# Layer 3's convolution, gate, u and u·B of 28 of 32 chunks placed between layer 1's tiles

## The chip, the cores and the metric

The kernel runs on one NeuronCore of a Trainium2 chip. Its engines work side by side, each through its own instruction stream in order: TensorE (PE, with its weight loads PEld), VectorE (DVE), ScalarE (ACT), GpSimd (POOL), and SyncE (SP), which here only issues DMAs. Times are device microseconds (us) of whole executions, the median of several, and one more execution is taken by the hardware profiler. Lower is better.

## The reference

Four layers are applied in turn to x of shape (4, 64, 64, 128): four images of 4096 pixels with 128 channels, all in float32.

```python
# layer 0: neighbourhood attention (7x7 windows, 4 heads of 32), gated, plus x
# layer 1: group norm, then attention of all 4096 pixels over all 4096, plus x
h = group_norm(x, gn_scale, gn_bias); hf = h.reshape(B, N, C)
q, k, v = hf @ wq + bq, hf @ wk + bk, hf @ wv + bv
w_ = softmax(einsum('bqd,bkd->bqk', q, k) * C ** -0.5, axis=2)
x = x + (einsum('bqk,bkd->bqd', w_, v) @ wo + bo)
# layer 2: per pixel, with one sum over each image row
out = ((x @ W_left + b_left) + (x @ W_eq + b_eq)) * sum_over_row(x @ W_right + b_right)
x = layer_norm((out * sigmoid(x @ W_gate + b_gate)) @ W_out + b_out + x)
# layer 3: a gated scan in four directions over 256 channels
xb, z = split(x @ Win)                     # 256 and 256 channels
xb = silu(depthwise_conv3x3(xb) + conv_b)  # u of the scan
xs = stack([xf, xf[::-1], xt, xt[::-1]])   # rows, rows backwards, columns, columns backwards
dt, Bs, Cs = split(xs @ Wxproj)            # 8, 1 and 1
delta = softplus(dt @ dt_weight + dt_bias)
x_t = exp(delta*A) * x_(t-1) + delta*u*B;  y_t = x_t*C + u*D
out = norm((y0 + y1 + y2 + y3) * silu(z)) @ Wout
```

## The kernel before, in words

`layers_0_to_2` (L91) takes one image b after the other. `layer_0(b)` is a generator that does the neighbourhood attention block by block; the additive masks for windows (`bias_m`, three tiles for inner rows of blocks, and an edge tile tagged "be" for the first and last row of blocks) stay in SBUF, and `edge_bias(0)` for the next image is loaded when layer 0 of this one has ended. `layer_1(b)` (L483) does the attention over all pixels in 32 tiles of 128 queries. In the turn of tile i it does four things. `soften(i-1)` takes the maximum of the previous tile's scores: three halvings on DVE (L554), a transpose on PE (L556), a reduction (L558), a diagonal (L560), a broadcast by PE (L562), the subtraction on DVE (L565) and the exponential on ACT (L566). `score(i)` does 8 groups of 4 matmuls (L542) into one of four PSUM buffers (tag "s"), each copied to SBUF by ACT (L545), with running maxima on DVE (L547, L549). `value(i-2)` (L572) multiplies the exponentials with v, its groups alternating with the scores on PE. `finish(i-2)` (L576, L577) divides by the sum.

After each tile `between(i)` (L677) is called. From i = 6 on it does a quarter of a chunk of layer 2: chunk n and part are `divmod(i - 6, 4)`, the parts being `turn`, `mix`, `add` and `norm`, and a chunk is four tiles, 512 pixels. `norm` stores the chunk's result, transposed, to DRAM (`x3_d`, L663). After layer 1's last tile, four more turns end layer 2 while the next image's layer 0 starts.

`layer_3` (L693) begins when all images are done. For each of 32 chunks (4 images of 8) `project` (L807 to L816) loads x from `x3_d` ("x3T"), multiplies it with Win into xb (copied to SBUF by ACT) and z (Silu on ACT, stored to `zf_d`). `convolve` (L817 on) forms the 3x3 convolution in PSUM: three of the nine taps on PE as matmuls with weights that were multiplied with the taps beforehand (L825), six on DVE as multiply-adds onto PSUM (L832). ACT applies Silu to it (u, L837), and D·u goes into the accumulators `zs` through ACT and POOL (L841 to L845). Every fourth chunk multiplies u with Wxproj (L851), which gives dt, B and C ("dbl"). u·B is formed by `times_b` (L882), on POOL an image later, on DVE for the last image, and goes to `ub_d`. The scan stage follows: `deltas` (L937, L945, L947), exponentials (L957) and the scans (L971), then the output stage.

Instructions are put in order by a scheduler; those in `keep_in_program_order` (or `pin`) keep the written order. Each engine then runs its stream in order. All DMAs that are issued with `nc.sync` share SP's stream: one that waits for data holds up those after it. What the numbers of the profile call L556 or L832 are lines of the code below.

Of the kernel before, what the change touches and what calls it, by code (L numbers as in the profile page):

```python
# [29 lines left out]
P = 128  # L30
# [35 lines left out]


@with_exitstack
def conv_seq(ctx, tc, x, mata, matb, cols, rows, rpb, dtw, convw, sel, out):
    nc = tc.nc  # L70
    xf = x.rearrange("b h w c -> b (h w) c")
    of = out.rearrange("b h w c -> b (h w) c")

    dram = ctx.enter_context(tc.tile_pool(name="dram", bufs=1, space=DRAM))
    const = ctx.enter_context(tc.tile_pool(name="const", bufs=1))
    x3_d = [dram.tile([P, L], F32, name=f"x3_d{b}") for b in range(B)]

    ident = const.tile([P, P], F32, name="ident")
    make_identity(nc, ident)
    col = const.tile([P, NCOL], F32, name="col")  # L80
    nc.sync.dma_start(col, cols)

    def cl(name, i=0, n=1, p=P):
        a = COL[name][0] + i
        return col[0:p, a:a + n]

    layers_0_to_2(tc, xf, mata, rows, rpb, ident, cl, dram, x3_d)
    layer_3(tc, of, matb, dtw, convw, sel, ident, cl, dram, x3_d)


@with_exitstack  # L91
def layers_0_to_2(ctx, tc, xf, mata, rows, rpb, ident, cl, dram, x3_d):
    nc = tc.nc
# [59 lines left out]
    for cv, n in enumerate(cols_of):  # L153


        runs = [(0, BC, 0, 3)] if cv == 1 else [(3, BC - 3, 0, 3)] if cv == 0 else [(0, BC - 3, 0, 3)]
        if cv == 0:
            runs += [(q, 1, 0, KS - 1 - q) for q in range(3)]
        if cv == 2:
            runs += [(q, 1, 12, BC - 1 - q) for q in range(BC - 3, BC)]  # L160
        nd = HEADS * (2 * KS - 1)
        for q, count, k, r in runs:
            dst = bass.AP(t_d[cv].tensor, t_d[cv].offset + q * nd * n + k, [[nd * n + 1, count], [n, nd], [1, KS]])
            src = bass.AP(rpb.tensor, rpb.offset + r, [[0, count], [2 * KS - 1, nd], [1, KS]])
            dma(dst, src)


# [89 lines left out]

    bias_m = [wp.tile([P, HEADS * 14 * n], F32, name=f"bias_m{k}") for k, n in enumerate(cols_of)]
    first_edge = edge_bias(0)
# [10 lines left out]
    def layer_0(b, xt, edge_t):  # L270
# [207 lines left out]
        handed[b] = hT, st  # L478
        if b + 1 < B:
            edge_of[b + 1] = edge_bias(0)  # L480

# [121 lines left out]
    def layer_2(b, xt):  # L603
# [61 lines left out]
        return turn, mix, add, norm  # L665

    coming = layer_0(0, x_next, edge_of[0])
    ahead = [x_next]
    for b in range(B):
# [5 lines left out]
        def between(i):  # L675
# [4 lines left out]
            if i >= 6 and n < NCH:  # L680
                parts[part](n)

        layer_1(b, xt, *handed.pop(b), between)
        if b + 1 < B:
# [8 lines left out]
@with_exitstack  # L693
def layer_3(ctx, tc, of, matb, dtw, convw, sel, ident, cl, dram, x3_d):
    nc = tc.nc
# [5 lines left out]

    def stored(name):
        return [[dram.tile([P, L], F32, name=f"{name}{b}_{f}") for f in range(2)] for b in range(B)]

    ub_d, zf_d, y_d = stored("ub_d"), stored("zf_d"), [stored("yn_d"), stored("yt_d")]
    z_d = [dram.tile([P, L], F32, name=f"z_d{f}") for f in range(2)]
    bc_d = [[dram.tile([1, L], F32, name=f"bc_d{b}_{r}") for r in range(3)] for b in range(B)]

# [3 lines left out]

    dbl = wp.tile([P, L], F32, name="dbl")
    dt = wp.tile([P, DI], F32, name="dt")
    nc.sync.dma_start(dt, dtw)
# [47 lines left out]

    RC = CH // W
    taps_pe = [(0, 0), (0, -1), (0, 1)]
    taps_ve = [(-1, 0), (-1, -1), (-1, 1), (1, 0), (1, -1), (1, 1)]
    with pool("u", 22) as up, pool("z") as zp, pool("a", 2) as ap, pool("psB", 2, space=PSUM) as psp:


        zs = [zp.tile([P, L], F32, name=f"zs{f}") for f in range(2)]
        for f in range(2):
            nc.vector.tensor_scalar(
# [23 lines left out]
        xbs = [ap.tile([P, H, W], F32, name=f"xb{f}", tag=f"xb{f}", bufs=1) for f in range(2)]  # L798
        us, bbs = {}, {}

        def region(n, dy, dx):

            return max(0, -dy - RC * n), min(RC, H - dy - RC * n), max(0, -dx), min(W, W - dx)

        def project(b, n):
            x = ap.tile([P, RC, W], F32, name="x3T", tag="x3T", bufs=6)
            nc.sync.dma_start(x, by_rows(x3_d[b][:, bass.ts(n, CH)]))  # L807
            for f in range(2):
                pi = psp.tile([P, RC, W], F32, name="pi", tag="i")
                nc.tensor.matmul(pi, lhsT=mb[:, win + P * f:win + P * f + P], rhs=x, start=True, stop=True)  # L810
                nc.scalar.copy(xbs[f][:, RC * n:RC * n + RC, :], pi)
                pz = psp.tile([P, RC, W], F32, name="pz", tag="i")
                nc.tensor.matmul(pz, lhsT=mb[:, win + DI + P * f:win + DI + P * f + P], rhs=x, start=True, stop=True)
# [5 lines left out]
        def convolve(b, n, x):  # L819
            for f in range(2):  # L820
# [18 lines left out]
                zv = at(zs[f], b, CH * n, CH * n + CH)  # L839
                if b == 0:  # L840
                    nc.scalar.activation(zv, by_rows(u), AF.Copy, scale=d)  # L841
                else:
                    du = ap.tile([P, CH], F32, name="du", tag="du")
                    nc.scalar.activation(du, u, AF.Copy, scale=d)
                    nc.gpsimd.tensor_tensor(zv, zv, by_rows(du), ALU.add)  # L845
            if n % 4 == 3:
# [8 lines left out]
                for g in range(4):  # L855
                    nc.scalar.copy(
                        dbl[32 * b:32 * b + NDBL, bass.ts(n - 3 + g, CH)], pd[32 * g:32 * g + NDBL, :]
                    )
                if b == B - 1:

                    o = 32 * b
                    for g in range(4):
                        pb = psp.tile([P, CH], F32, name="pb3", tag="d")
                        nc.tensor.matmul(
                            pb, lhsT=pick[o:o + NDBL, 0, :], rhs=dbl[o:o + NDBL, bass.ts(n - 3 + g, CH)],
                            start=True, stop=True,
                        )
                        times_b(b, n - 3 + g, pb, nc.vector)
            if n == NCH - 1:
                for r in range(2):  # L870
                    row = 32 * b + RANK + r
                    nc.sync.dma_start(bc_d[b][r], dbl[row:row + 1, :])
                nc.sync.dma_start(cts[b][:, 0, :], by_rows(bc_d[b][1])[0])
                if b < B - 1:
                    turn_c(b, psp.tile([W, W], F32, name="pt3", tag="d"))
                    bbs[b] = zp.tile([P, L], F32, name="bb3", tag="bb3")
                    nc.sync.dma_start(bbs[b], bc_d[b][0][0].partition_broadcast(P))

# [5 lines left out]

        chunks = [(b, n) for b in range(B) for n in range(NCH)]
        xs = {0: project(0, 0)}
        for j, (b, n) in enumerate(chunks):
            if j + 1 < len(chunks):
                xs[j + 1] = project(*chunks[j + 1])
            convolve(b, n, xs.pop(j))  # L890
            if b > 0:
                times_b(b - 1, n, bbs[b - 1][:, bass.ts(n, CH)], nc.gpsimd)
            if (b, n) == (1, NCH - 1):
                load_ub(ub_s[0], 0, 0)
                load_c(cb_s[0], 0, 0)
        for f in range(2):
# [320 lines left out]
```

## Time and profile before

| | |
|---|---|
| median of 3 runs | 3924.59 us (3923.41 to 3926.62) |
| profiled execution: time | 3926.75 us |
| profiled execution: span | 3925.0 us |
| mean granted PE clock | 0.916 |
| layer 1 of images 0 to 3 starts at | 236.5, 954.0, 1673.6, 2392.8 us |
| four tiles of layer 1 with layer 2's parts | 64.40 us |
| layer 3: first x3T lands, first scan | 2924.0, 3276.1 us |
| ACT, Silu 128x512 (L837); SBUF to SBUF 128x512 (L844) | 0.685; 0.723 us |
| ACT, copy of scores 128x512 (L545); load of a function table | 0.585; 1.283 us |
| DVE, tap 128x512 onto PSUM (L832) | 0.745 us |
| DVE, maximum 128x512 (L554) alone; while POOL is in a sum | 0.69; 1.65 us |
| POOL, product 128x512 (L882); sum into turned rows (L845) | 1.29; 1.52 us |
| PE, one record of a float32 matmul of 512; of 128 columns | 0.427; 0.113 us |

The span is what lies between the first and the last instruction that the profiler recorded; the time of an execution contains a little more, here 1.75 us. A float32 matmul shows as two records. "Idle before" an instruction is time in which its engine had nothing to run, and the releaser is what it was waiting for. The "chain that ended last" goes back from the last instruction through what released each one.

### The profile page before, as it was taken

To read this page: it belongs to the slowest core of one execution; us is meant where nothing else is said; L and a number is where in the kernel's file an instruction comes from. 1 tells how busy PE (TensorE), PEld (TensorE's weight loads), DVE (VectorE), ACT (ScalarE), POOL (GpSimd) and SP (SyncE) were. 2 spreads that over 40 slices of the span, in tenths; PEclk is the share of its full clock that TensorE was granted. 3 is DMA by queue.
4 is the path that set the end of the run, shared out by engine and by line. 5 is a ranking of instruction groups with operands and counts; after the bars stand their busy time and mean duration, and the time that the engine had idled before them with its cause. 6 is when DMAs were issued, how large, how long until landed. Compare 5 with 4: busy or idle time off the path is not lost.

```text
span 3925.0 us, 68131 instructions
## 1 busy us (share of the span) xinstructions
PE 3549.6 (90%) x26648; PEld 2823.9 (72%) x26648; DVE 2811.4 (72%) x4974; ACT 2504.0 (64%) x4066; POOL 1101.9 (28%) x1267
## 2 busy tenths in 40 slices
PE   7999999999999999999999999999989996665647
PEld 4689999767999996699999668999973332222236
DVE  3657777665777765567777565777768887998978
ACT  4855566586566557755665685556645557988944
POOL 5500000152000005300000350000001646887866
PEclk8999999999999999999999999999999995555569
DMA  4100000110000002100000110000013546998998
GB/s 124 37 15 25 4 6 4 37 49 21 23 7 4 6 7 67 33 17 10 7 4 7 55 34 1 4 4 6 4 52 121 215 148 193 280 268 254 263 274 289
DMA packets 172471, 292.31 MB, mean 74 GB/s; under 512 B 18287, under 2 KB 104844, under 8 KB 165356
## 3 DMA queue, kind: packets, MB, share of 16 engines
q1 hardware_dynamic: 128388, 210.65, 15.3%
q0 software_dynamic: 15168, 51.78, 6.9%
q10 hardware_dynamic: 28592, 25.51, 1.9%
q8 instruction: 210, 3.44, 0.4%
q14 instruction: 113, 0.93, 0.1%
HBM read 163.15 MB, written 91.25 MB: 65 GB/s over the span
## 4 chain that ended last, share of the span: by engine, by line
PE 60%; DVE 19%; ACT 9%; DMA 4%; issue 4%; POOL 3%; SPq 0%; DVEq 0%; POOLq 0%; ACTq 0%
PE sc L542 17%; PE po L572 17%; PE pc L825 3%; DVE st L565 3%; DVE mx L554 3%; DVE mx L549 3%; PE pt L424 3%; DMA y<-yo 2%; ACT st L566 2%; PE sc L389 2%; PE po L435 2%; ACT pr L407 2%; POOL inp L947 2%; DVE h L971 2%; PE pi L810 1%
## 5 line engine op out<-in xcount | busy, mean ns | idle before, releaser
L572 PE MATMUL po<-v,st 128*128 128x129 f32 x8192 | 1090.0, 274 | 2.9 <-ACT st L566 2.9
L542 PE MATMUL sc<-qT,kT 128*128 128x128 f32 x8192 | 1083.2, 275 | 0.0
L545 ACT COPY st<-sc 128x512 f32<-128x512 f32 x1024 | 583.3, 585 | 713.0 <-PE sc L542 706.1
L572 PEld LDWEIGHTS po<-v,st 128*128 128x128 f32 x8192 | 1006.4, 192 | 6.2 <-issue 4.2
L542 PEld LDWEIGHTS sc<-qT,kT 128*128 128x128 f32 x8192 | 998.0, 192 | 11.5 <-issue 11.5
L565 DVE TENSOR_TENSOR st<-st,pb 128x2048 f32<-128x2048 f32 x256 | 575.5, 2282 | 73.2 <-PE pb L562 73.2
L549 DVE TENSOR_TENSOR mx<-mx,st 128x1024 f32<-128x1024 f32 x256 | 313.7, 1225 | 286.0 <-ACT st L545 280.7
L566 ACT ACTIVATE st<-st 128x2048 f32<-128x2048 f32 x256 | 483.6, 1910 | 43.0 <-DVE st L565 42.4
L631 POOL TENSOR_TENSOR x<-x,row 128x512 f32<-128x512 f32 x32 | 49.8, 1555 | 1596.6 <-PE pt L211 1596.6
L937 PE MATMUL pdt<-dbl,dt 8*128 8x512 f32 x512 | 307.8, 1088 | 174.0 <-ACT de L945 172.3
L937 PEld LDWEIGHTS pdt<-dbl,dt 8*128 8x128 f32 x512 | 114.3, 314 | 366.2 <-ACT de L945 303.1
L947 POOL TENSOR_TENSOR inp<-de,ub 128x1024 f32<-128x1024 f32 x128 | 357.7, 2961 | 64.1 <-ACT de L945 62.1
L415 POOL TENSOR_SCALAR pr<-pr,sm 128x308 f32<-128x308 f32 (+3 forms) x512 | 244.6, 497 | 261.8 <-DVE sm L413 194.8
L832 DVE SCALAR_TENSOR_TENSOR pc<-xb,cc,pc 128x504 f32<-128x504 f32 (+3 forms) x384 | 263.6, 739 | 52.5 <-PE pc L825 36.9
L407 ACT ACTIVATE pr<-pr,mx 128x308 f32<-128x308 f32 (+3 forms) x512 | 262.5, 516 | 0.0
L547 DVE TENSOR_TENSOR mx<-st 128x1024 f32<-128x1024 f32 x128 | 156.5, 1223 | 109.4 <-ACT st L545 109.4
L971 DVE TENSOR_TENSOR_SCAN h<-h,end,inp 128x1024 f32<-128x1024 f32 x96 | 220.7, 2344 | 8.3 <-ACT h L957 6.0
L424 PE MATMUL pt<-ident,pr 128*88 128x128 f32 (+5 forms) x1472 | 205.1, 276 | 7.9 <-ACT prT L426 7.8
L554 DVE TENSOR_TENSOR mx<-mx 128x512 f32<-128x512 f32 (+2 forms) x384 | 204.9, 534 | 6.2
L393 DVE CUSTOM_DVE_ANT_0 pr<-sc,bias_m 128x266 f32<-128x266 f32 (+1 forms) x384 | 151.7, 451 | 67.7 <-PE sc L389 62.6
L424 PEld LDWEIGHTS pt<-ident,pr 128*88 128x88 f32 (+5 forms) x1472 | 164.2, 138 | 45.7 <-ACT prT L426 31.6
L426 ACT COPY prT<-pt 110x512 f32<-110x512 f32 (+3 forms) x240 | 139.1, 580 | 76.0 <-PE pt L424 75.9
(212 smaller groups left out, 4941.2 us busy)
## 6 DMA issues: line engine op xcount, KB each, us to landing
cb<-bc_d SPq DMA_DIRECT2D x16, 2048.0 KB
y<-yo POOLq DMA_DIRECT2D x64, 512.0 KB, 12.3
zf_d<-zf ACTq DMA_DIRECT2D x64, 256.0 KB
ub_d<-u SPq DMA_DIRECT2D x64, 256.0 KB
ub<-ub_d SPq DMA_DIRECT2D x16, 1024.0 KB
y<-z_d POOLq DMA_DIRECT2D x32, 512.0 KB, 8.2
yn_d<-y SPq DMA_DIRECT2D x32, 512.0 KB
yl<-yn_d SPq DMA_DIRECT2D x64, 256.0 KB
```

The source lines that it names most:

```text
L407: pin(nc.scalar.activation(k.pr[:, h], k.pr[:, h], AF.Exp, bias=k.mx[:, h:h + 1], accum_out=k.sm[:, h:h + 1]))
L424: pin(nc.tensor.transpose(pt[0:n, h, :], k.pr[:, h, at:at + n], ident))
L542: nc.tensor.matmul(ps[:, r, :], lhsT=kT[:, bass.ts(G * g + r, P)], rhs=qT[:, bass.ts(i, P)], start=True, stop=True)
L545: nc.scalar.copy(k.st[:, G * g:G * g + G, :], ps)
L549: nc.vector.tensor_tensor(k.mx, k.mx, k.st[:, 4 * g - 4:4 * g + 4, :], ALU.max)
L554: nc.vector.tensor_tensor(mx[:, 0:n, :], mx[:, 0:n, :], mx[:, n:2 * n, :], ALU.max)
L565: nc.vector.tensor_tensor(part, part, pb.unsqueeze(1).to_broadcast([P, 16, P]), ALU.add)
L566: nc.scalar.activation(part, part, AF.Exp)
L572: nc.tensor.matmul(k.po, lhsT=k.st[:, j, :], rhs=v[:, j, :], start=(j == 0), stop=(j == NT - 1))
L937: nc.tensor.matmul(pdt[j][:, g, :], lhsT=dt[o:o + RANK, P * f:P * f + P], rhs=at(dbl[o:o + RANK, :], k & 2, g0, g0 + CH), start=True, stop ...
L947: nc.gpsimd.tensor_tensor(by_rows(inp), by_rows(de), at(ub, b ^ (k & 1), SC * n, SC * n + SC), ALU.mult)
L971: nc.vector.tensor_tensor_scan(h[:, way], h[:, way], inp[:, way], prev, ALU.mult, ALU.add)
```

## The change

A new function `front(b)` inside `layers_0_to_2` takes on layer 3's first stage for 28 chunks. `between(i)` calls its `turn(i)` after layer 2's part. During image b's layer 1, turns 0 to 15 do chunks 4 to 7 of image b-1, and turns 16 to 31 do chunks 0 to 3 of image b: four turns for one chunk. Turn r = 0 projects to xb (PE, ACT copies into `xh`, which has a row more above and below) and begins the accumulator on ACT with the middle tap and `conv_b`. Turns 1 and 2 add four taps of one half each on DVE. In every turn ACT multiplies two of the four corner taps into tiles tagged "xT", of which there are two, and POOL adds them in the next turn. Turn 3 computes the gate, stores it and loads the next chunk's x. Four turns on, `activate` applies Silu (in the turn of the next chunk's gate); a turn later `lower` makes D·u (stored to `du_d`, for odd images by a POOL DMA that adds), multiplies with Wxproj in four groups of 32 columns, stores dt, B, C to `dbl_d` and reads B back, broadcast; and a turn later `times_b` multiplies u with B on POOL and stores it to `ub_d`. Turn 31 needs one row of the chunk after: `project_row`.

No tap is on PE in these chunks; the nine are one on ACT alone, four on DVE, and four on ACT with POOL. SBUF room comes from the masks: `acc0`, `acc1`, `u` and `xh` share slots with `bias_m` and the edge tile, so the masks are copied to DRAM once (`bias_d`), and read back after each image's layer 1; `edge_bias(0)` moves there too. Layer 3 then keeps the last four chunks of image 3 in the old form (with `times_b` on DVE), and begins with loads of dbl, of the stored D·u (`zs` and `zt`, added by POOL), of `ub_0` and of C.

```diff
+    taps_ve = [(-1, 0), (1, 0), (0, -1), (0, 1)]
+    taps_gp = [(-1, -1), (-1, 1), (1, -1), (1, 1)]
+    def front(b):
+        xh = wp.tile([P, 2, 2, RC + 2, W], F32, name="xh", tag="be")
+        accs = [wp.tile([P, 2, CH], F32, name=f"acc{k}", tag=f"bm{2 * k}") for k in range(2)]
+        u = wp.tile([P, 2, CH], F32, name="u0", tag="bm1")
...
+        def project(i, n):
+            me = n & 1
+            for f in range(2):
+                pi = ps_s([P, CH], "pi")
+                nc.tensor.matmul(pi, lhsT=win[:, P * f:P * f + P], rhs=x_of[i, n], start=True, stop=True)
+                nc.scalar.copy(xh[:, me, f, 1:RC + 1, :], by_image_rows(pi))
...
+        def gate(i, n):
+            x = x_of.pop((i, n))
+            for f in range(2):
+                pz = ps_s([P, CH], "pz")
+                nc.tensor.matmul(pz, lhsT=win[:, DI + P * f:DI + P * f + P], rhs=x, start=True, stop=True)
+                zf = tmp.tile([P, CH], F32, name="zf", tag="c512", bufs=9)
+                tc.keep_in_program_order(nc.scalar.activation(zf, pz, AF.Silu))
+                nc.sync.dma_start(zf_d[i][f][:, bass.ts(n, CH)], zf)
...
+        def begin(n, f):
+            acc, x, c = tap(n, f, 0, 0)
+            nc.scalar.activation(acc, x, AF.Identity, bias=cl("conv_b", f), scale=c)
+        def multiply(n, f, dys):
+            for dy, dx in dys:
+                acc, x, c = tap(n, f, dy, dx)
+                p = by_image_rows(tmp.tile([P, CH], F32, name="tp", tag="xT"))[:, 0:acc.shape[1], 0:acc.shape[2]]
+                nc.scalar.activation(p, x, AF.Copy, scale=c)
+                parts_of.append((acc, p))
+        def add_parts():
+            for acc, p in parts_of:
+                nc.gpsimd.tensor_tensor(acc, acc, p, ALU.add)
+            parts_of.clear()
+        def add_taps(n, f):
+            for dy, dx in taps_ve:
+                acc, x, c = tap(n, f, dy, dx)
+                nc.vector.scalar_tensor_tensor(acc, x, c, acc, ALU.mult, ALU.add)
+        def activate(n):
+            tc.keep_in_program_order(nc.scalar.activation(u, accs[n & 1], AF.Silu))
+        def lower(i, n):
+            lo, hi = CH * n, CH * n + CH
+            for f in range(2):
+                du = tmp.tile([P, CH], F32, name="du", tag="c512", bufs=9)
+                nc.scalar.activation(du[:, ::-1] if i & 1 else du, u[:, f, :], AF.Copy, scale=cl("d", 2 * i + f))
+                if i & 1:
+                    nc.gpsimd.dma_start(du_d[i >> 1][f][:, L - hi:L - lo], du, accum_op=ALU.add)
+                else:
+                    nc.sync.dma_start(du_d[i >> 1][f][:, lo:hi], du)
+            pd = ps_t([P, P], "pd")
+            for f in range(2):
+                for g in range(4):
+                    nc.tensor.matmul(
+                        pd[HD * g:HD * g + HD, :], lhsT=wx[:, f, :], rhs=u[:, f, bass.ts(g, P)],
+                        start=(f == 0), stop=(f == 1),
+                    )
+            dq = tmp.tile([P, P], F32, name="dq", tag="gb")
+            nc.scalar.copy(dq, pd)
+            for g in range(4):
+                nc.sync.dma_start(dbl_d[i][:, lo + P * g:lo + P * g + P], dq[HD * g:HD * g + NDBL, :])
+            bb = x_of[i, n, "b"] = tmp.tile([P, CH], F32, name="bb0", tag="c512", bufs=9)
+            nc.sync.dma_start(bb, dbl_d[i][RANK:RANK + 1, lo:hi][0].partition_broadcast(P))
+        def times_b(i, n):
+            bb = x_of.pop((i, n, "b"))
+            for f in range(2):
+                nc.gpsimd.tensor_tensor(u[:, f, :], u[:, f, :], bb, ALU.mult)
+                nc.sync.dma_start(ub_d[i][f][:, bass.ts(n, CH)], u[:, f, :])
...
+                if now:
+                    if r == 0:
+                        begin(now[1], 0)
+                        begin(now[1], 1)
+                    if r in (1, 2):
+                        add_taps(now[1], r - 1)
+                    multiply(now[1], r // 2, taps_gp[2 * (r & 1):2 * (r & 1) + 2])
+                if r == 3:
+                    for c in takes[j]:
+                        gate(*c)
+                    for c in takes[j + 1] if j < 7 else []:
+                        load(*c)
+            for k, c in enumerate(whole):
+                at = 4 * k + 7 if k < 7 else 33
+                if c:
+                    if i == at:
+                        activate(c[1])
+                    if i == at + 1:
+                        lower(*c)
+                    if i == at + 2:
+                        times_b(*c)
...
+    for t, d in zip(bias_m, bias_d):
+        nc.sync.dma_start(d, t)
     coming = layer_0(0, x_next, edge_of[0])
...
+            first_part(i)
+            if b + 1 < B and i == NT + 1:
+                edge_of[b + 1] = edge_bias(0)
+            if b + 1 < B and i == NT + 3:
+                bias_m[:] = bias_tiles()
+                for t, d in zip(bias_m, bias_d):
+                    nc.sync.dma_start(t, d)
...
         zs = [zp.tile([P, L], F32, name=f"zs{f}") for f in range(2)]
+        for f in range(2):
+            zt = zp.tile([P, L], F32, name="zt", tag=f"zt{f}")
+            nc.sync.dma_start(zs[f], du_d[0][f])
+            nc.sync.dma_start(zt, du_d[1][f])
+            nc.gpsimd.tensor_tensor(turned(zs[f]), turned(zs[f]), by_rows(zt), ALU.add)
...
+        load_ub(ub_s[0], 0, 0)
+        load_c(cb_s[0], 0, 0)
+        for b in range(B - 1):
+            nc.sync.dma_start(cts[b][:, 0, :], by_rows(bc_d[b][1])[0])
+            turn_c(b, psp.tile([W, W], F32, name="pt3", tag="d"))
+        b = B - 1
+        xs = {n: project(b, n) for n in (3, 4)}
+        for n in range(4, NCH):
+            if n + 1 < NCH:
+                xs[n + 1] = project(b, n + 1)
+            convolve(b, n, xs.pop(n))
```

## The prediction

> **What bounds the kernel now.** I read the page's row of busy times first, then the table of windows for a stretch of layer 1 and for layer 3, then the waits and the timeline inside layer 1. The page:
>
> ```profile
> span 3925.0 us, 68131 instructions
> PE 3549.6 (90%) x26648; PEld 2823.9 (72%) x26648; DVE 2811.4 (72%) x4974; ACT 2504.0 (64%) x4066; POOL 1101.9 (28%) x1267
> ```
>
> TensorE (PE) is the bound on average, but the change moves work between two stages, so each needs its own row. The columns are the stretch, then busy us (count) of PE, PE's weight loads, DVE, ACT and POOL, then PE's clock, the DMA share and GB/s. The first two are groups of four tiles of layer 1, the third layer 3's convolution, the last the beginning of its scan:
>
> ```profile
> 1062.60:1127.00 64.40, 63.39 (x548) 61.66 (x547) 47.62 (x67) 39.06 (x48) 2.65 (x2) 1.00 0.02 5
> 1127.00:1191.40 64.40, 63.39 (x548) 61.66 (x547) 47.62 (x67) 39.07 (x48) 2.65 (x2) 1.00 0.01 5
> 2924.00:3276.10 352.10, 339.08 (x810) 127.89 (x811) 274.33 (x403) 189.35 (x300) 138.98 (x100) 0.94 0.45 167
> 3276.10:3400.00 123.90, 80.83 (x132) 29.45 (x129) 113.75 (x90) 113.37 (x100) 104.56 (x57) 0.50 0.83 220
> ```
>
> In layer 1 PE is busy 98%, with 1.0 us of 64.40 free; whatever is added to PE there lengthens it one for one. DVE is at 74%, ACT at 61%, POOL at 4%: room on average, but these engines feed PE through a short loop: ACT's copy of scores (L545), DVE's maxima (L549, L554), PE's transpose (L556). Its slack is small, as the waits of five such groups (1062 to 1385 us) show:
>
> ```profile
> PEld pt L556 <- DVE mx L554: 6.7, 10, 1.1
> PE pt L556 <- DVE mx L554: 4.5, 5, 0.9
> ```
>
> Once in four tiles PE already waits about a microsecond for DVE. The timelines of DVE and POOL show why:
>
> ```profile
> 1109.91 1.65 DVE L554 TENSOR_TENSOR mx<-mx 128x512 f32<-128x512 f32 x1
> ```
>
> ```profile
> 1109.41 1.60 POOL L631 TENSOR_TENSOR x<-x,row 128x512 f32<-128x512 f32 x1 [43.96 <-PE pt L211]
> ```
>
> A maximum that takes 0.69 us alone (100 of 128) takes 1.65 when POOL is inside a two-operand sum.
>
> [...] DVE operations with a PSUM operand (L565, L832) show no second duration. It matters because the moved taps have two SBUF operands where L832's accumulator lay in PSUM. [...] row L435 shows 24 records of 32 columns in 0.86 us.
>
> **The change, part by part.** Layer 1's four images run from 236, 954, 1674 and 2393 us. A chunk is 512 columns of an image; chunks 0 to 3 go between their image's last tiles, 4 to 7 between the next image's first; image 3's last four stay.
>
> *Removed from layer 3.* Before, the stage is 352 us. The first x3T lands at 2924.0, the first product is at 2928.6, the first scan (L971) at 3276.1. Afterwards four chunks remain. They keep this course: 4.6 us to the first product plus one chunk's projection (3), 4 × 12 STT (L832) × 0.745 = 36, and the tail of today's last chunk (last u 3250.6 to scan 3276.1) 25.5: 70 us. Their x3T loads stand in SP's queue behind 8 MB of stored D·u, 4 MB of u·B and C, and 0.4 MB of weights; big loads move 370 to 435 GB/s here, so 12.4/0.40 = 31 us after the queue opens. It opens about where x3T was issued, 2919; the last chunk's lowering adds nothing if it is done by then, 10 if not. So x3T lands at 2950 to 2960, the scan at 3020 to 3030: I take 3030, a gain of **246**. Bounds: 230 (turned sums on POOL, 4096 wide, 8 × 1.5 to 3 us, come in the way) to 260.
>
> *Added to PE.* Per chunk two pi and two pz (512 columns, two records of 0.427 each): 4 × 0.854 = 3.4. The lowering with 32 columns: 16 records, 0.57 by L435; without overlap of column groups 1.81. 4.0 × 28 = **+112** (to 147).
>
> *Start and transitions.* The copy of the masks to DRAM (1.7 MB) and layer 3's weights (0.3 MB) are issued on SP ahead of layer 0's v, whose first load stands in the chain at 54.5 us: 2 MB at 0.4 MB/us is 5 us, and SP has to wait at that copy until the masks are filled, 4 by my estimate: **+9** (0 to 15). At each of three image changes, edge and masks are read back (3.1 MB, 8 us) once chunk 3 has freed their slots, behind writes that wait in SP's queue; layer 0's first scores need them, and half of it is covered by the last tiles: 4 each, **+12** (0 to 30).
>
> *The other engines, per group.* ACT: 2 copies 1.17, 2 beginnings 1.45, 8 products 5.8, 2 gates 1.2, one Silu of 1024 about 1.1, 2 D·u 1.45, dq 0.26, two table loads 2.6, row and edge work 0.5: 15.5, so 54.6 of some 70 us (78%). DVE: 8 STT × 0.745 = 6, plus lock losses: 75 to 80%. POOL: 8 sums at 1.3 to 1.5, 2 products with B at 1.29, edge copies: 2.65 becomes about 17. None reaches PE's 68.4, so averages give no cost; order does. On ACT the products of the taps stand ahead of the next tile's score copies and need POOL to have emptied one of two buffers; POOL's sums add to the accumulator after DVE's taps, and its product with B waits for dbl to go to DRAM and return (about 2.5 us each way). A late POOL thus holds ACT, ACT holds the score copy, that holds PE's four score banks. On DVE the four taps stand ahead of maxima that PE's transpose waits for: 3 us in front of a loop that lost 1 us to a single contention. Following one group, I find PE waiting 0.2 to 1.5 at the transpose after projection, 0.4 for a bank at pz, 2.4 to 3 at the next tile's transpose, less the 1.0 idle that exists: 2 to 4. I take 3. From below it is zero (everything fits between tiles); from above each of 8 POOL sums and 2 products blocks a maximum by about 1 us, with half reaching PE, and the ACT-POOL-DVE chain adds 3: 8. 3 × 28 = **+84**.
>
> *Sum.* 3926.8 (profiled execution; 1.8 is outside its span) − 246 + 112 + 9 + 12 + 84 = 3898. The median of the runs is 2 below the profiled execution: **3896**.
>
> **Rivals.** *Stalls are hidden* (0.5 us per group, 14 in all): 3896 − 70 = 3826. For it: DVE, ACT and POOL all have a quarter or more free. Against it: PE already waits for L554 with only one POOL sum in its way, and there will be ten.
> *The lock and the in-order queues decide* (the other side): with 6 or more per group, 168 in all, 3896 + 84 = 3980. Its place is transpose L556 (L588 in the changed kernel) behind L554 and the score copy L545. Break-even is where stalls take (246 − 112 − 21)/28 = 4.0 us per group; only 1 above what I take. For it: 1.65 against 0.69 for a locked maximum, and three in-order engines in one ring. Against it: several of the locked operations fall where PE has four banks of scores in hand.
> *Layer 3's beginning does not shrink*: bandwidth, not PE, sets it. The loads moved in front are 12.4 MB and the scan stage already holds DMA at 0.83. If x3T lands only when all of it and POOL's sums are done, the gain is 200: 3942.
> *The change isn't what it says* is excluded by the order of instructions: all 28 chunks' matmuls stand between layer 1's.
>
> **How the numbers follow.** Likeliest, stalls 1.5 to 4 per group: 0.48, its own range 3855 to 3930. Hidden: 0.12, 3810 to 3855. Lock decides: 0.36, 3930 to 4010. Layer 3's beginning: 0.04. What a measurement tells from no change is 0.2%, 8 us: 3917 to 3932. Of the likeliest case 0.08 falls inside and 0.40 below; hidden adds 0.12 below: faster 0.52. Same 0.10 with 0.02 from the third. Slower: 0.34 + 0.04 = 0.38. For 8 in 10 I cut half of the hidden case and the top of the lock's: 3840 to 3985.
>
> **What would show it.** Right: a group of four tiles with a chunk at 70 to 73 us; PE's idle before the transpose up from 1 to about 4 us a group, released by DVE's maxima; L554's mean above today's 0.53; ACT near 78% there; layer 3's x3T at 2950 + the shift of layer 1, and the first scan 70 us after it. Wrong: PE's records of the lowering at 1.8 us; a group of 68 to 69 us (hidden) or over 74 (lock or ring decides; then waits on POOL's sums should stand in ACT's row); waits for the masks' reload at the image changes above 10 us; a first scan more than 90 us after x3T.

## The result and the profile after

The changed kernel takes 4022.78 us (median of 4 runs, 4016.59 to 4024.18), against 3925.61 us (4 runs) for the kernel before on the same chip: a ratio of 1.0245, 95% interval 1.0227 to 1.0263. It is slower by 97 us; 3896 was forecast, and the range ended at 3985. The profiled execution has a span of 4021.2 us, 96.2 longer than before. The page's first rows, of the changed kernel:

```profile
span 4021.2 us, 68983 instructions
PE 3445.2 (86%) x26660; PEld 2818.7 (70%) x26660; DVE 2796.2 (70%) x4854; ACT 2699.4 (67%) x4364; POOL 1464.2 (36%) x1535
```

PE is busy 104 us less than before (3549.6), and the kernel is nevertheless longer: PE now waits. Where, the windows tell. First the whole of layer 1 of the second image before, from its first to its last score, in the columns used above (stretch, busy us of PE, its weight loads, DVE, ACT, POOL, then PE's clock, DMA share, GB/s):

```profile
954.00:1446.30 492.30, 484.62 (x4193) 472.81 (x4192) 362.30 (x480) 296.93 (x362) 17.52 (x13) 1.00 0.03 9
```

The same stretch of the changed kernel, then its layer 1 of the first image, its change from image 0 to 1, and the time from layer 1's last value to the first scan:

```profile
1013.90:1585.10 571.20, 529.34 (x4357) 497.83 (x4356) 425.32 (x544) 391.38 (x509) 140.00 (x106) 0.98 0.11 35
245.10:777.60 532.50, 507.91 (x4261) 486.66 (x4261) 393.32 (x512) 343.65 (x434) 75.06 (x56) 0.98 0.07 23
777.60:1013.90 236.30, 215.20 (x1977) 148.79 (x1975) 129.04 (x487) 162.48 (x436) 94.55 (x201) 0.95 0.18 56
3229.10:3371.70 142.60, 73.08 (x185) 29.79 (x184) 48.63 (x88) 42.84 (x62) 53.68 (x22) 0.67 0.58 203
```

Layer 1 of the second image became 78.9 us longer. PE's busy time rose by 44.7 us for only 164 more records, and its free time from 7.7 to 41.9. No engine is full: ACT is at 69%, DVE at 74%. And PE's clock is no longer 1.00 but 0.98. The waits over the same stretch (engine and line, what it waited for: us in total, times, longest) name the ring of engines:

```profile
PEld pt L588 <- DVE mx L586: 45.2, 29, 4.5
PE pt L588 <- DVE mx L586: 38.7, 21, 4.4
POOL acc L773 <- DVE acc L779: 36.2, 9, 8.1
ACT tp L768 <- POOL acc L773: 33.6, 38, 2.6
```

PE waits at the transpose for DVE's maxima, ACT for POOL, POOL for DVE. A group of four tiles with its chunk takes 74.7 to 75.5 us at the end of this stretch, where it took 64.4 before: past the 74 that the prediction gave as the sign that the lock or the ring decides, and ACT's waits for POOL's sums, its other sign, are there too. (The lock is a name for what the traces show: here a running maximum, L581, takes 1.23 us alone, and 1.91 at the median of the 73 that lie beside one of POOL's sums, 2.32 at most.) One such wait in the timeline, in the order PE, DVE, ACT, POOL (start, us, then in brackets the idle time before it and its releaser):

```profile
1477.49 1.06 PE L604 MATMUL po<-v,st 128*128 128x129 f32 x8
1481.98 0.33 PE L588 MATMUL pt<-ident,mx 128*128 128x128 f32 x1 [3.43 <-DVE mx L586]
...
1473.86 2.10 DVE L581 TENSOR_TENSOR mx<-mx,st 128x1024 f32<-128x1024 f32 x1
1478.34 1.23 DVE L581 TENSOR_TENSOR mx<-mx,st 128x1024 f32<-128x1024 f32 x1 [2.30 <-ACT st L577]
1480.46 1.47 DVE L586 TENSOR_TENSOR mx<-mx 128x512 f32<-128x512 f32 x3
...
1474.91 0.72 ACT L768 ACTIVATE tp<-xh,cc 128x504 f32<-128x504 f32 x1 [0.41 <-POOL acc L773]
1477.12 0.71 ACT L768 ACTIVATE tp<-xh,cc 128x504 f32<-128x504 f32 x1 [1.49 <-POOL acc L773]
1477.74 0.57 ACT L577 COPY st<-sc 128x512 f32<-128x512 f32 x1
...
1471.41 7.01 POOL L773 TENSOR_TENSOR acc<-acc,tp 128x504 f32<-128x504 f32 x4 [3.22 <-DVE acc L779]
```

Read backwards from 1481.98: the transpose needs L586, L586 stands behind the last running maximum (L581 at 1478.34), which needs the score copy of 1477.74. That copy was queued on ACT behind a product (1477.12) that waited for one of two buffers, and POOL empties them at 1.75 us each in a row of four sums, having waited for DVE's taps. Meanwhile L581 at 1473.86, begun while POOL is in one of these sums, takes 2.10 us instead of 1.23.

The clock of 0.98 has a cause of its own. The profile's clock records switch between full and half at steps of 3.41 us. In the second image's layer 1 eight such steps are at half clock, 30 over the four images, and none before. PE need not be wholly idle for it, as the last section shows. In such a step the score records follow one another 0.213 us apart at the median, in the others 0.112. If each costs half of 3.41 us, that is 30 × 1.707 = 51 us of matmuls that are only slower. PE's records say the same by another way: over the four layers 1 PE is busy 160.0 us longer than before, and 109.4 longer in a run below with the same matmuls and no step at half clock; the difference is 50.6.

The span's 96.2 us, by stretches of the two traces:

| term | forecast | measured | from |
|---|---|---|---|
| start, to layer 1 of the first image | +9 | +8.6 | 236.5 to 245.1 |
| layer 1: PE's added work | +112 | +109.4 | the run without POOL's sums, below |
| layer 1: PE free | +84 | +118.6 | 4 × 7.7 = 30.8 to 24.6 + 41.9 + 42.0 + 40.9 |
| layer 1: half clock | 0 | +51 | 30 steps × 1.707 |
| three image changes | +12 | +37.3 | 225.3, 227.3, 226.9 to 236.3, 241.0, 239.5 |
| last value to first scan | −246 | −229.2 | 371.8 to 142.6 |

They add up to 95.7, and the time after the first scan is 0.5 longer. Layer 1 as a whole, from first score to last, is 278.7 longer where 196 was forecast.

### The profile page after: what moved, and what is told of

Its sections match the earlier page's. It is cut to its first block, busy times and chain, and to the rows that moved or that the text cites. A ratio compares the mean times of both kernels' runs of the same rounds, so it can differ in the third digit from the quotient of the medians.

```text
span 4021.2 us, 68983 instructions
## 1 busy us (share of the span) xinstructions
PE 3445.2 (86%) x26660; PEld 2818.7 (70%) x26660; DVE 2796.2 (70%) x4854; ACT 2699.4 (67%) x4364; POOL 1464.2 (36%) x1535
## 5 line engine op out<-in xcount | busy, mean ns | idle before, releaser
L604 PE MATMUL po<-v,st 128*128 128x129 f32 x8192 | 1107.2, 278 | 2.8 <-ACT st L598 2.8
L574 PE MATMUL sc<-qT,kT 128*128 128x128 f32 x8192 | 1104.6, 279 | 0.7 <-ACT st L577 0.7
L574 PEld LDWEIGHTS sc<-qT,kT 128*128 128x128 f32 x8192 | 1018.4, 195 | 16.0 <-issue 13.3
L604 PEld LDWEIGHTS po<-v,st 128*128 128x128 f32 x8192 | 1023.6, 195 | 6.1 <-issue 5.3
L597 DVE TENSOR_TENSOR st<-st,pb 128x2048 f32<-128x2048 f32 x256 | 573.8, 2282 | 74.5 <-PE pb L594 74.5
L581 DVE TENSOR_TENSOR mx<-mx,st 128x1024 f32<-128x1024 f32 x256 | 357.3, 1396 | 283.6 <-ACT st L577 279.3
L773 POOL TENSOR_TENSOR acc<-acc,tp 128x504 f32<-128x504 f32 (+1 forms) x224 | 349.8, 1563 | 460.6 <-ACT acc L762 205.9
L598 ACT ACTIVATE st<-st 128x2048 f32<-128x2048 f32 x256 | 482.8, 1909 | 34.9 <-DVE st L597 34.2
L768 ACT ACTIVATE tp<-xh,cc 128x504 f32<-128x504 f32 (+1 forms) x224 | 157.7, 711 | 117.1 <-POOL acc L773 112.6
L586 DVE TENSOR_TENSOR mx<-mx 128x512 f32<-128x512 f32 (+2 forms) x384 | 217.4, 566 | 6.4
L659 POOL TENSOR_TENSOR o<-o,rt 128x512 f32<-128x512 f32 x32 | 34.0, 1061 | 462.4 <-DVE o L658 462.2
```

Source lines behind the costliest of these rows:

```text
L574: nc.tensor.matmul(ps[:, r, :], lhsT=kT[:, bass.ts(G * g + r, P)], rhs=qT[:, bass.ts(i, P)], start=True, stop=True)
L581: nc.vector.tensor_tensor(k.mx, k.mx, k.st[:, 4 * g - 4:4 * g + 4, :], ALU.max)
L597: nc.vector.tensor_tensor(part, part, pb.unsqueeze(1).to_broadcast([P, 16, P]), ALU.add)
L598: nc.scalar.activation(part, part, AF.Exp)
L604: nc.tensor.matmul(k.po, lhsT=k.st[:, j, :], rhs=v[:, j, :], start=(j == 0), stop=(j == NT - 1))
L773: nc.gpsimd.tensor_tensor(acc, acc, p, ALU.add)
```

## The experiments

The kernel before was timed beside each of these, at 3922 to 3930 us, so that differences between two experiments are good to a few us. A ratio is to the kernel before. "Idle" is PE's free time in layer 1 of the second image (7.7 before, 41.9 in the changed kernel), "half steps" the clock steps at half in the four layers 1 (0 and 30).

**The order of the transpose.** In `layer_1`, the halvings stay ahead of the scores, and the rest of `soften` comes later:

```diff
-                soften(blocks[i - 1])
+                halve(blocks[i - 1])
...
             for g in range(NT // G):
+                if g == 3 and 0 < i <= NT:
+                    soften(blocks[i - 1])
```

> The changed kernel, with the transpose, broadcast and exponential of the tile before placed after three groups of scores instead of ahead of them. Theory (PE loses time because it stands at the transpose while ACT's score copies and DVE's maxima are late, and it has other work ready): PE's idle time in layer 1 of images 1 to 3 falls from 42 us to under 15 each, the clock there returns to 1.00, time 3880 to 3930 us. Rival (ACT, DVE and POOL as a ring are simply too slow for a group, wherever PE waits): the wait moves to the values that need the exponentials, time 3990 or more.

Measured: 4037.86 us, ratio 1.0295 (1.0277 to 1.0313), idle 44.6, half steps 36. PE now waits little at the transpose; in 570 us (1150 to 1720), these are the waits there and at the broadcast after it:

```profile
PE pb L598 <- DVE dm L596: 23.3, 11, 5.2
PEld pb L598 <- DVE dm L596: 14.9, 8, 3.7
...
PE pt L592 <- DVE mx L587: 5.8, 3, 4.4
```

The wait moved on to where DVE has to answer again, and the kernel became 15 us slower. My theory that order was at fault fell: PE meets the late engines at the next place.

**Without corner taps**, in the turn:

```diff
-                    multiply(now[1], r // 2, taps_gp[2 * (r & 1):2 * (r & 1) + 2])
```

> The changed kernel without the four corner taps between tiles (ACT's products and POOL's sums are left out, so 4 of 9 taps are missing in 28 chunks). Theory (ACT's products wait for POOL, POOL for DVE, and the score copies stand behind them): the waits of 3.4 to 4.2 us at the transpose fall to about 1, clock 1.00 in layer 1, time 3880 to 3920 us. Rival (DVE's own four taps ahead of the maxima make the wait): PE's idle time in layer 1 stays above 30 us an image, time above 3970.

Measured: 3849.98 us, ratio 0.9807 (0.9792 to 0.9821), idle 8.4, no half step. This is 173 us less than the changed kernel, and below what was expected: the corner taps account for nearly all of PE's free time and for the clock too. The window of its second image's layer 1:

```profile
991.00:1515.10 524.10, 515.66 (x4357) 486.56 (x4356) 404.59 (x544) 349.27 (x443) 40.29 (x42) 1.00 0.12 37
```

DVE's own four taps, the middle tap on ACT, gates and lowering between the tiles cost hardly more than PE's own work. Hence the second term of the table: the four layers 1 are longer than before by 111.4 us here and by 110.8 in the kernel with ACT's products alone, of which 2.8 and 1.5 are idle, so that 108.6 and 109.4 are PE's work.

**All taps on DVE**, with the corners among `taps_ve` and four taps of one half in each turn:

```diff
-    taps_ve = [(-1, 0), (1, 0), (0, -1), (0, 1)]
+    taps_ve = [(-1, 0), (1, 0), (0, -1), (0, 1), (-1, -1), (-1, 1), (1, -1), (1, 1)]
...
-                    multiply(now[1], r // 2, taps_gp[2 * (r & 1):2 * (r & 1) + 2])
+                    add_taps(now[1], r // 2, taps_ve[4 * (r & 1):4 * (r & 1) + 4])
```

> The changed kernel with all eight outer taps on DVE, four of one half in each turn, nothing of the taps on POOL and only the middle one on ACT. Theory (the ring through POOL is the cause): waits at the transpose of 1 to 2.5 us each, now from DVE alone, time 3920 to 3980 us. Rival (DVE's load is what counts): 6 us more on DVE a group makes it slower than the changed kernel, above 4025.

Measured: 3851.50 us, ratio 0.9814 (0.9800 to 0.9829), idle 8.5, no half step. The work is the whole work, the time is below what the theory expected (3920 to 3980), and the kernel beats the one before by 73 us. The window of its second image's layer 1:

```profile
986.90:1511.00 524.10, 515.61 (x4357) 486.46 (x4356) 437.33 (x608) 348.08 (x443) 38.87 (x42) 1.00 0.12 37
```

DVE is at 83% here, against 74% in the changed kernel, and PE waits hardly more than before: it does the same 4357 records in 515.6 us where it took 529.3, since the clock is whole. The rival, DVE's load, is out: with eight taps on DVE the kernel takes 1.5 us more than with no corner taps at all.

**Which part of the ring: five cuts.** The first two take one partner away. ACT's products without POOL's sums:

```diff
                 nc.scalar.activation(p, x, AF.Copy, scale=c)
-                parts_of.append((acc, p))
```

> The changed kernel with ACT's eight products of the corner taps but without POOL's sums of them (the corner taps are missing from 28 chunks). It shows what ACT's 5.8 us a chunk cost alone. If the wait for POOL makes the stalls: PE's idle time in layer 1 under 12 us an image, time 3850 to 3870 us. If ACT's load ahead of the score copies makes them: idle 20 to 30 us, time 3900 to 3930.

Measured: 3850.18 us, idle 8.0, no half step. ACT's 5.8 us a chunk (the prediction's estimate) cost nothing that these runs tell.

POOL's sums without ACT's products (`p` and its product are gone, `parts_of` gets `(acc, x)`):

> The changed kernel with POOL's eight sums, but of the projected chunk itself onto the accumulator, without ACT's products (the corner taps enter unscaled and undisplaced in 28 chunks). [...] If the lock alone makes the stalls: idle 25 us or more an image, time above 3910. If the ring needs ACT: idle under 15 us, time 3850 to 3880.

Measured: 3969.85 us, ratio 1.0107, idle 35.5, 18 half steps. The sums alone bring 120 of the 173 us. The expectation that the ring needs ACT failed.

The sums may hold DVE up in two ways: by the accumulator that both write, and by the lock. With neither ACT nor the accumulator:

```diff
...
-                nc.gpsimd.tensor_tensor(acc, acc, p, ALU.add)
+                q = by_image_rows(tmp.tile([P, CH], F32, name="tp", tag="xT"))[:, 0:acc.shape[1], 0:acc.shape[2]]
+                nc.gpsimd.tensor_tensor(q, p, p, ALU.add)
```

> The changed kernel without ACT's products and with POOL's eight sums reading only the projected chunk and writing to tiles that nobody reads (no corner taps in 28 chunks): [...] If the lock alone holds DVE's maxima up: idle in layer 1 of 15 to 30 us an image, time 3890 to 3930. If it takes the shared accumulator or ACT: idle under 10 us, time 3845 to 3860.

Measured: 3943.10 us, ratio 1.0048 (1.0032 to 1.0065), idle 30.8, 7 half steps: above what was expected of the lock alone. More than half of the loss, 93 us, comes with sums whose results nobody reads and that wait for nothing of DVE's accumulator. The window of its second image's layer 1, in which ACT is as little busy as without corner taps:

```profile
999.20:1551.10 551.90, 521.10 (x4357) 490.00 (x4356) 432.19 (x544) 349.06 (x443) 114.88 (x106) 0.99 0.11 35
```

The groups of DVE's taps (count, busy us, mean ns; idle before), here and then with ACT alone, where POOL is still:

```profile
L778 DVE SCALAR_TENSOR_TENSOR acc<-xh,cc,acc 128x504 f32<-128x504 f32 (+2 forms) x224 | 225.8, 1014 | 2.0 <-POOL xh L731 0.6
```

```profile
L778 DVE SCALAR_TENSOR_TENSOR acc<-xh,cc,acc 128x504 f32<-128x504 f32 (+2 forms) x224 | 163.8, 735 | 2.3 <-POOL xh L731 0.6
```

A tap with two SBUF operands goes from 735 to 1014 ns, 62 us in all; half of them take 746 or less, the longest 1758. In the table of waits, nothing of ACT or DVE waits for POOL in the second image by more than 0.2 us, so the delay lies within the taps. That it is a lock, and not two engines that slow each other down in proportion, the ends of the operations show. Two pairs:

```profile
1219.41 1.37 POOL L772 TENSOR_TENSOR tp<-xh 128x441 f32<-128x441 f32 x1
1220.01 1.30 DVE L778 SCALAR_TENSOR_TENSOR acc<-xh,cc,acc 128x504 f32<-128x504 f32 x1
1289.28 1.18 POOL L772 TENSOR_TENSOR tp<-xh 128x504 f32<-128x504 f32 x1
1289.58 1.42 DVE L778 SCALAR_TENSOR_TENSOR acc<-xh,cc,acc 128x512 f32<-128x512 f32 x1
```

Of the 224 taps 89 took over a tenth longer than alone, and each of the 89 overlaps an operation on POOL. In 86 of them that operation had begun first, and the tap ended 0.54 to 0.55 us after it, whether 0.76 us of it had been left or 1.2. So the tap waited for POOL's end; at a shared pace that distance would grow with what had been left. In the changed kernel the taps are not stretched (734 ns on average), since there they and the sums wait for one another on the accumulator (POOL for DVE 129.4 us over the kernel, DVE for POOL 23.9), and none began inside a sum; the running maxima are:

```profile
L581 DVE TENSOR_TENSOR mx<-mx,st 128x1024 f32<-128x1024 f32 x256 | 357.3, 1396 | 283.6 <-ACT st L577 279.3
```

That mean is 1224 ns with ACT alone: 44 us of DVE's time over the kernel.

The other two keep ACT and POOL and loosen one tie. Sums of each product to itself, off the accumulator (`nc.gpsimd.tensor_tensor(p, p, p, ALU.add)`):

> The changed kernel, with each of POOL's sums adding a product to itself instead of to the accumulator (the corner taps are missing from the result of 28 chunks; the number, size and buffers of the operations are unchanged). Theory A (POOL's sums wait for DVE's taps on the same accumulator, and pass that wait on to ACT): idle in layer 1 under 20 us an image, time 3870 to 3920 us. Theory B [...]: idle above 30 us, time above 3980.

Measured: 3928.82 us, ratio 1.0006 (0.9998 to 1.0015), idle 27.0, 4 half steps. Between both theories, of which B puts the loss down to the lock and to POOL's own pace: without the shared accumulator 94 us of the loss are gone, 79 remain. But the edit does one thing more. A sum of a tile with itself is shorter: 1.03 us at the median here and 1.02 in the kernel with the lock alone, against 1.26 in the changed kernel, each where no maximum or tap ran on DVE at its start. So both runs also make POOL's operations shorter.

Products in nine shared buffers instead of two (`tag="c512", bufs=9`):

> The changed kernel, with the corner products in the group of nine buffers that layers 0 and 2 use for chunks instead of in two of their own. Theory 1 (ACT stands because a product finds neither of two buffers free): ACT no longer waits for POOL, PE's idle time in layer 1 of images 1 to 3 falls from 42 us to under 20, time 3870 to 3920 us. Theory 2 (POOL is slow and locks DVE, whatever the buffers): idle stays above 30, time above 3980.

Measured: 3966.84 us, ratio 1.0108 (1.0093 to 1.0123), idle 34.2, 13 half steps. ACT's waits for POOL's sums are gone from the table of waits there, and 56 us with them; 117 remain. The idle time is as theory 2 had it, the total between the two.

The five don't add up as a sum would, but they put bounds: with POOL's sums in place the loss is 79 to 173 us, without them none. Without the shared accumulator, and with shorter sums, it is 93 and 79. With the accumulator but without ACT's tie to two buffers it is 120 (no products) and 117 (nine buffers). All ties together make 173. So the lock needs no partner, and the two buffers are worth 53 to 56 us where POOL's sums also wait for DVE's accumulator, since a late sum then makes a late product and a late score copy. How the rest divides is open: each cut also shifts which DVE operations the sums collide with.

**Layer 3's beginning.** The loads of x3T and `cw` are issued ahead of `zs` and `zt`:

```diff
+        x3s = {}
+        for n in range(3, NCH):
+            x3s[n] = ap.tile([P, RC, W], F32, name="x3T", tag="x3T", bufs=6)
+            nc.sync.dma_start(x3s[n], by_rows(x3_d[B - 1][:, bass.ts(n, CH)]))
+        cw = ap.tile([P, 3, DI], F32, name="cw", tag="cw", bufs=1)
+        nc.sync.dma_start(cw, convw[3:6].partition_broadcast(P))
         zs = [zp.tile([P, L], F32, name=f"zs{f}") for f in range(2)]
...
```

> The changed kernel with the loads of x3T and of the tap weights issued ahead of the 12 MB of stored products, u B and C in layer 3. Theory (x3T waits in SP's queue behind them): the first tap comes about 25 us earlier, the first scan 15 to 25 us, unless the sums of zs on POOL then come late; time 3998 to 4010 us. Rival (the loads all have to come anyway before the scan): the first scan moves by under 5 us, time 4018 to 4025.

Measured: 3984.49 us, ratio 1.0152 (1.0137 to 1.0167): 38 us less than the changed kernel, and more than the theory expected. Last value to first scan is 112.8 us, from 142.6; the rest of the 38 is scattered (the time after the first scan is 4 us shorter), and I don't explain it. DVE's first taps in layer 3, in the changed kernel and then here:

```profile
3311.17 9.40 DVE L1044 SCALAR_TENSOR_TENSOR pc<-xb,cc,pc 128x512 f32<-128x512 f32 x12 [21.88 <-PE pc L1037]
```

```profile
3278.56 9.40 DVE L1047 SCALAR_TENSOR_TENSOR pc<-xb,cc,pc 128x512 f32<-128x512 f32 x12 [6.52 <-PE pc L1040]
```

So x3T's place in the queue was the cause, and bandwidth wasn't: what is loaded stays the same, and the scan begins 30 us earlier.

**Both together**: all taps on DVE, and x3T first.

> All eight outer taps on DVE, together with x3T's loads first in layer 3. If the two effects are independent (171 us and 38 us): 3805 to 3820 us. If the first scan is then held by the sums of zs on POOL or by bandwidth: 3830 to 3850.

Measured: 3821.03 us, ratio 0.9733 (0.9719 to 0.9748), 1 above the range. The two effects are nearly independent.

**The image changes.** In the changed kernel, at the first of them (PE, ACT):

```profile
804.75 1.08 PE L797 MATMUL pd<-u,wx 128*32 128x128 f32 x16 [6.73 <-ACT u L782]
...
802.34 1.28 ACT L782 ACT_TABLE_LOAD   x1 [3.70 <-DMA ub_d<-u]
```

There is one tile for u. The last chunk's Silu can't write it until the chunk before has been multiplied with B, which comes by way of DRAM, and stored. Between tiles there are four turns for that, at the end of an image two. So for the two last chunks of each image's turn B comes from PE:

```diff
...
-            bb = x_of.pop((i, n, "b"))
+            dq = bb = x_of.pop((i, n, "b"))
+            if n in (2, 3):
+                bb = ps_t([P, CH], "pb0")
+            for g in range(4 if n in (2, 3) else 0):
+                nc.tensor.matmul(bb[:, bass.ts(g, P)], lhsT=pick[:, g:g + 1].to_broadcast([P, P]), rhs=dq, start=True, stop=True)
             for f in range(2):
-                nc.gpsimd.tensor_tensor(u[:, f, :], u[:, f, :], bb, ALU.mult)
+                (nc.vector if n in (2, 3) else nc.gpsimd).tensor_tensor(u[:, f, :], u[:, f, :], bb, ALU.mult)
```

> The kernel just named, with B of the last two chunks of each image's turn broadcast by four matmuls of PE from dq and multiplied on DVE out of PSUM, instead of by way of DRAM and POOL. Theory (the image changes lose 11 to 14 us because u of the last chunk waits for the round trip of B and the store of u B of the one before): each change 5 to 9 us shorter, 15 to 25 us less than the kernel just named. Rival (reading back the masks and edges is what costs): less than 5 us.

Measured: 3806.52 us, ratio 0.9700 (0.9684 to 0.9716), 14.5 less than both together. The three changes take 27.5 us more than before, from 35.7, and last value to first scan goes from 112.0 to 107.1. That is just under what the theory expected in all, and 2.7 us a change where it expected 5 to 9: B's way explains a quarter of what the changes lost. PE's wait for u is still 5.3 us at each of them.

The clock makes up most of the rest. In the changed kernel PE's waits for u at the three changes are 6.7, 8.6 and 6.5 us, 21.9 together. PE was busy for 63.5 us at half clock there, against 31.7 before; half of the 31.8 more is 16 us. The two come to the 37.3 us of the table within 1 us. Other terms are small or cancel. With B from PE the waits for u are 15.8, from 18.9 in the kernel just before it, and PE's time at half clock is 44.6, from 65.1.

**The start.** As the last, with the copy of the masks to DRAM in the sixth turn of layer 1 of the first image:

> Taps on DVE, x3T first, B of the two last chunks by PE, and the copy of the masks to DRAM issued in the sixth turn of layer 1 of the first image instead of ahead of layer 0. Theory (SP stands at that copy until the masks are filled): layer 1 begins 4 to 8 us earlier, 3798 to 3803 us. Rival (the weights' loads and not the copy cost the start): no more than 1 us, 3805 to 3808.

Measured: 3805.45 us, ratio 0.9690 (0.9674 to 0.9706). Layer 1 begins 3.3 us earlier in the trace, less than the theory expected; in the medians it is 1 us, as the rival had it, which the runs (3802.12 to 3808.30) don't tell from nothing. With either of these two, moving 28 chunks into layer 1 is worth about 120 us.

## Why the prediction was wrong

The forecast for the span was 29 us less than before, and it became 96 more. Of the 125 between, the stalls are 35, the clock in layer 1 51, the image changes 25 and layer 3's beginning 17; PE's added work gives 3 back.

*PE's added work* (112): right, 109.4. The records of the lowering took 1.08 us where 16 run with the clock down, 0.65 otherwise; the bound of 1.81 didn't come.

*Stalls* (3 us a group, 84): this is the step that failed. Measured are 118.6/28 = 4.2 us of free time and 51/28 = 1.8 of half clock, 6.1 together, which is above the break-even of 4.0. Most of the mechanism was the one described: maxima held up by the lock, POOL's sums behind DVE's taps, and ACT's products ahead of the score copies. But its size was put at 3 us, from a single group followed by hand with each operation at its length alone or a locked length once, and 6 and more was left to a rival. That rival had the place right, the transpose. Its 6 us was reached only with the clock, which it didn't mention. One part of the mechanism was wrong: the four taps on DVE ahead of the maxima, for which the prediction counted 3 us in front of the loop. With them and without corner taps PE's free time in the second image is 8.4 us, and with eight taps 8.5, where it was 7.7 before. My upper bound of 8 us a group held.

*The clock* (no term): missed. The page showed a clock of 1.00 throughout layer 1, and I read it as given. It follows how busy PE was in the step before, as the last section's counts show, and so the wait of 3.43 us shown above cost 1.7 us more than itself. This is 51 us in layer 1, the largest part of the miss, and about 16 more in the image changes.

*Image changes* (12): the reading back of masks, which I priced, isn't what the waits show; the wait for u, which I didn't price, and the clock are. 37.3 measured.

*Layer 3's beginning* (246): 229 measured. The queue as the cause and the tail of 70 us were right: the first scan is 60.6 us after the first tap, 3311.2 to 3371.8. But the first tap was due 64 us after the last value (x3T 56, then 7.6), and came 82 after it. SP issued the first load of the stored D·u here:

```profile
3261.39 0.33 SPq L984 DMA_DIRECT2D zs<-du_d  x1
```

That is 32 us after the last value, where I had taken 15, the time of before: SP's stream held the last chunks' stores until then. x3T is there for its first product at 3298.3, 37 us later, where 31 were worked out and 41 taken, and the first tap came 13 us after that instead of 7.6. So what was mis-sized is mainly the time until SP's queue opens, by 17 us. The gain of 200 in the rival was too low, the lower bound of 230 is what came.

*Start* (9): the number was right, 8.6, but only 3.3 of it is traced to SP's copy; the rest isn't shown, and the agreement may be luck.

What would have changed the forecast: not the averages, which again leave every engine free, but asking of each added operation on POOL which DVE operation with two SBUF operands is on PE's loop at that time. The change adds ten POOL operations of this kind to a group, and one of the two that were there had already cost PE a microsecond.

## What to carry to other kernels

Before giving work to an engine that is nearly idle, look at what it shares. Here POOL was at 4%, and eight sums a chunk on it, fed by ACT, cost 173 us; the same taps on DVE, already at 74%, cost 1.5 us, since they wait for no product, no sum and no buffer of another engine. And price a wait of TensorE also by how much of a 3.41 us step it empties. The wait of 3.43 us shown above, which ends at 1481.98, is followed by a step at half clock from 1482.5 on, which costs 1.7 us more.

## What the runs showed of the hardware

*Half clock has a sharp edge.* Over the layers 1 of 14 traces (before, changed, and the twelve experiments; the first 7 us of each left out), PE's clock fell to half 107 times. I compared each step with how busy PE had been in the 3.41 us before. It fell after steps with PE busy for 0.46 of them or less, and at no step in which it had been busy for 0.47 or more; it stayed whole at none below 0.44. In the changed kernel alone it fell 23 times, after steps with PE busy for 0.02 to 0.39, and stayed whole after none below 0.54. PE need not be idle for the fall: only 5 of the 107 came after a step in which it was busy for less than 0.02. By the edge at 0.47, as an estimate, a single wait of up to 1.8 us can't empty a step of 3.41 us that far (1.8/3.41 is 0.53), but two of 1.2 and 1.1 us close together did (busy for 0.34, in the run with the later transpose), and so did single waits of 2.0 us. By the same estimate a wait of 3.4 us does, unless a border between steps cuts it near the middle. The time adds up: PE's busy time in the second image's layer 1 is 13.7 us longer than with all taps on DVE for the same number of records, and 8 × 1.707 is 13.7.

*The way back has another edge.* Of the 138 steps at half clock, 31 were followed by another at half, all after PE had been busy for 0.79 or less; the clock became whole after the other 107, in which it had been busy for 0.84 or more. So a fall can cost two steps: the 30 steps in the changed kernel come from 23 falls.

*The lock spares neither side.* Of POOL's 224 sums in the changed kernel, 91 began while a running maximum, a halving or a tap was under way on DVE. They have a median of 2.12 us and end 1.12 us after that operation at the median; the other 133 have a median of 1.26 us. On the other side, 85 running maxima there began inside one of POOL's sums, and the 70 of them that had more than 0.11 us of it ahead ended 1.08 to 1.09 us after its end, whether 0.19 us of it had been left or 1.24; alone such a maximum takes 1.23. DVE's tap goes from 735 to 1014 ns on average beside sums that it has nothing else to do with. Operations of DVE with an operand in PSUM show no such delay: in the changed kernel the subtraction (L597) takes 2.28 us at the median, in the 58 that lie beside a sum as in the 198 others, and before, the tap of 504 columns onto PSUM (L832) takes 0.744 beside a sum or product of POOL and 0.743 otherwise.
